# A kernel that multiplies each sample by its subject's matrix: how the eight matrices are loaded

## The chip, the cores and the metric

The kernel runs on one core of a Trainium2 chip. The metric is the device time of one execution in microseconds (us). The profile is of one execution, taken by the hardware profiler.

## The reference

There are 128 samples of 128 x 1024 floats, eight matrices of 128 x 128 floats, and for each sample the number of its subject. Each sample is multiplied by the matrix of its subject, and the sample itself is added:

```python
B, C, D, T, N_SUBJECTS = (128, 128, 128, 1024, 8)
w = weights[subjects]
out = jnp.einsum('bct,bcd->bdt', x, w)
x = x + out
```

All data are float32. The samples are 67 MB in and 67 MB out; the matrices are 0.5 MB, as much as one sample.

## The kernel before

Four samples (H x G, two halves of two) make a turn, and there are 32 turns. The memory on the chip holds 12 slots, `x_all`, of one turn each (2 MB); turn `i` uses slot `i % 12`. Every engine follows an order written out by hand, with semaphores between them.

**Loads.** ScalarE's queue issues all loads (L200 to L204), one DMA for each sample, through the helper `transfer` (L59). A load splits a sample's 512 KB into 32 runs of 16 KB: one run holds four rows of the sample (`ROWS`), and it goes to four partitions. From turn 12 on, ScalarE waits at L202 until the slot has been emptied, that is, until the store of the turn 12 before has landed. ScalarE computes nothing.

**The matrices.** SP's queue issues two DMAs at the start: the subjects' numbers (L180) and the matrices (L181). L181 reads `weights` as `s c d` and writes it as `c s d`: partition `c` gets row `c` of each of the eight matrices, so each run is one row, 512 B, and there are 1024 of them. VectorE waits for them at L222.

**Order of the compute.** VectorE prepares an index of the subjects (L193 to L199). For each half turn it copies the two matrices that are needed from `w_all` into `ws` (`place`, L153), and TensorE multiplies (`multiply`, L162) after a wait for the copies (L157) and one for the loads (L158). VectorE then adds the product to the sample in its slot (`add`, L174, after the wait at L173). TensorE and VectorE run their turns in loops (L226 and L231). GpSimd (L206 to L211) passes on to TensorE that a turn's loads have landed. At the start TensorE multiplies zeros (L186; six records in the profile).

**Stores.** SP waits at L213 until all loads of turn 7 (`AHEAD` is 8) have landed, and then stores turn after turn, each after a wait for its additions (L217). The last turn is stored in pieces, and the very last sample at L238.

Of the kernel before, what the change touches and what calls it, by code (L numbers as in the profile page):

```python
# [30 lines left out]
G = 2  # L31
H = 2
# [3 lines left out]
SLOTS = 12  # L36
# [5 lines left out]
DMA = 16  # L42

IDLE = 3

ROWS = 4

ALIGN = 4096
QUEUES = {mybir.EngineType.SP: "qSPDynamicHW", mybir.EngineType.Activation: "qActDynamicHW"}
# [2 lines left out]
def transfer(nc, engine, out, in_):  # L52

    later, nc._always_lower_symbolic_ap = nc._always_lower_symbolic_ap, False
    ins, outs = engine.lower_ap_dma(in_), engine.lower_ap_dma(out)
    nc._always_lower_symbolic_ap = later
    return engine.add_instruction(  # L59
        mybir.InstDMACopy(  # L60
            name=nc.get_next_instruction_name(),
            engine=engine.engine,
            ins=ins,
            outs=outs,
            mode="Copy",
            cce_op=ALU.bypass,
            queue=QUEUES[engine.engine],
        )
    )
# [3 lines left out]
def kernel(  # L73
# [7 lines left out]
    nc = tc.nc  # L81
    B, C, T = x.shape
    S, _, D = weights.shape
    NT = B // (G * H)

    def sbuf(name, *shape, dtype=F32):
        return ctx.enter_context(nc.sbuf_tensor(name, list(shape), dtype)).ap()
# [5 lines left out]
    x_all = sbuf("x_all", C, SLOTS * H * G * T)  # L93
# [1 line left out]
        x_all[:, i * H * G * T : (i + 1) * H * G * T].rearrange("c (q t) -> c q t", t=T)  # L95
        for i in range(SLOTS)
    ]
    w_all = sbuf("w_all", C, S, D)
    ws = [sbuf(f"w{i}", C, 1, D) for i in range(H * G)]
    zeros = sbuf("zeros", C, N)  # L100
    given, near, wrap = (sbuf(name, 1, B, dtype=I32) for name in ("given", "near", "wrap"))
# [3 lines left out]
    ]  # L105

    s_given = tc.alloc_semaphore("s_given")
    s_wall = tc.alloc_semaphore("s_wall")
    s_index = tc.alloc_semaphore("s_index")
    s_zeros = tc.alloc_semaphore("s_zeros")  # L110
# [9 lines left out]
    def emptied(i):  # L120
        turns = i // SLOTS
        return DMA * (H * G + 1) * turns - (DMA * G if i >= SLOTS and i % SLOTS == 0 else 0)

    def load(engine, i, q):
        transfer(
            nc,
            engine,
            xs[i % SLOTS][:, q, :],
            x[i * H * G + q].rearrange("(a r) t -> a (r t)", r=ROWS),
        ).then_inc(s_head if i * H * G + q < G else s_slot[i % SLOTS], DMA)  # L130

    def store(i, q0, q1):
        b = i * H * G
        transfer(
            nc,
            nc.sync,
            out[b + q0 : b + q1].rearrange("g d t -> d g t"),
            xs[i % SLOTS][:, q0:q1, :].rearrange("d (o g) t -> d o (g t)", g=min(G, q1 - q0)),
        ).then_inc(s_slot[i % SLOTS], DMA)

    def subjects_of(i):
        _, subject = nc.values_load_multi_w_load_instructions(
            index[0:1, i] if isinstance(i, slice) else index[0:1, bass.ds(i * (H * G), H * G)],
            engines=[mybir.EngineType.DVE],
            min_val=0,
            max_val=S - 1,
            skip_runtime_bounds_check_because="the index is clamped on the chip above",
        )
        return subject

    def place(h, subject):
        for q in range(h * G, (h + 1) * G):
            copy = nc.vector.tensor_copy(ws[q], w_all[:, bass.ds(subject[q], 1), :])  # L153
        copy.then_inc(s_go, 1)

    def multiply(slot, h):
        nc.tensor.wait_ge(s_go, 1).then_inc(s_go, -1)  # L157
        nc.tensor.wait_ge(s_ready, 1).then_inc(s_ready, -1)  # L158
        for q in range(h * G, (h + 1) * G):
            for t in range(0, T, N):  # L160
                at = slot * (H * G * T) + (q * T + t)
                mm = nc.tensor.matmul(  # L162
                    ps[h][:, q % G, t : t + N],
                    ws[q][:, 0, :],
                    x_all[:, bass.ds(at, N)],
                    start=True,
                    stop=True,
                )
        mm.then_inc(s_product, 1)

    def add(slot, h):
        mine = x_all[:, bass.ds(slot * (H * G * T) + h * G * T, G * T)]
        nc.vector.wait_ge(s_product, 1).then_inc(s_product, -1)  # L173
        nc.vector.tensor_tensor(  # L174
            mine, ps[h].rearrange("d g t -> d (g t)"), mine, ALU.add
        ).then_inc(s_added, 1)

    with tc.tile_critical():  # L178

        nc.sync.dma_start(given, subjects.rearrange("(o b) -> o b", o=1)).then_inc(s_given, DMA)  # L180
        nc.sync.dma_start(w_all, weights.rearrange("s c d -> c s d")).then_inc(s_wall, DMA)  # L181

        nc.vector.memset(zeros, 0.0).then_inc(s_zeros, 1)  # L183
        nc.tensor.wait_ge(s_zeros, 1)
        for _ in range(IDLE):
            nc.tensor.matmul(  # L186
                ps[P_SLOTS - 1][:, G - 1, :N], zeros[:, :D], zeros, start=True, stop=True
            )

        nc.vector.memset(index[:, B:], 0).then_inc(s_index, 1)  # L193
        nc.vector.wait_ge(s_given, DMA)
        nc.vector.tensor_scalar(near, given, -S, S - 1, ALU.max, ALU.min).then_inc(s_index, 1)  # L195
        nc.vector.wait_ge(s_index, 2)
        nc.vector.tensor_scalar(wrap, near, 0, S, ALU.is_lt, ALU.mult).then_inc(s_index, 1)  # L197
        nc.vector.wait_ge(s_index, 3)
        nc.vector.tensor_tensor(index[:, :B], near, wrap, ALU.add).then_inc(s_index, 1)  # L199
        for i in range(NT):  # L200
            if i >= SLOTS:
                nc.scalar.wait_ge(s_slot[i % SLOTS], emptied(i))  # L202
            for q in range(H * G):
                load(nc.scalar, i, q)  # L204

        for i in range(NT):  # L206
            if i == 0:
                nc.gpsimd.wait_ge(s_head, DMA * G).then_inc(s_ready, 1)
                nc.gpsimd.wait_ge(s_slot[0], DMA * G).then_inc(s_ready, 1)
            else:  # L210
                nc.gpsimd.wait_ge(s_slot[i % SLOTS], emptied(i) + DMA * H * G).then_inc(s_ready, H)  # L211

        nc.sync.wait_ge(s_slot[AHEAD - 1], DMA * H * G)  # L213
        for i in range(NT):
            for h in range(H):
                if i == NT - 1 or h == H - 1:
                    nc.sync.wait_ge(s_added, i * H + h + 1)  # L217
                    store(i, h * G if i == NT - 1 else 0, (h + 1) * G - (i * H + h == NT * H - 1))


        nc.vector.wait_ge(s_index, 4)
        nc.vector.wait_ge(s_wall, DMA)  # L222
        subject = subjects_of(slice(0, H * G))
        for h in range(H):
            place(h, subject)
        with nc.vector.Fori(0, NT) as turn:  # L226
            subject = subjects_of(turn + 1)
            for h in range(H):
                add(turn % SLOTS, h)
                place(h, subject)  # L230
        with nc.tensor.Fori(0, NT) as turn:  # L231
            for h in range(H):
                multiply(turn % SLOTS, h)
# [39 lines left out]
```

## Time and profile before

| | us |
|---|---|
| median of 3 runs | 323.39 |
| lowest and highest | 323.35, 323.67 |
| the profiled execution | 323.44 |
| its span, first to last instruction | 321.7 |
| TensorE's matmuls with samples (L162) | 239.6 busy |
| VectorE's additions (L174) | 146.7 busy, 2.29 each |
| VectorE's copies of matrices (L153) | 23.2 busy, 0.22 each |

The profile page has the span cut into 40 slices of 8 us, with each engine's busy share in tenths; the DMA rows have the mean busy share of the 16 DMA engines and what they moved. Windows give the same for any stretch of time. A line such as `ACTq L59 DMA_DIRECT2D ... x24` stands for 24 DMA issues by ScalarE's queue: its first number is when they began, the second how long they took together. q1 is SP's queue and q10 is ScalarE's. The trace also records every DMA packet, with its start, duration and size, and the times at which a transfer's semaphore increments landed; where the text speaks of packet records and landings, it means these.

### The profile page before, as it was taken

How to read it: one execution, taken by the hardware profiler on the slowest of the kernel's cores; microseconds unless marked ns; L12 is line 12 of the kernel's file. 1: busy time of each engine (PE TensorE's matmuls, PEld its weight loads, DVE VectorE, ACT ScalarE, POOL GpSimd, SP SyncE). 2: the span in 40 equal slices, each digit the busy share in tenths (PEclk: the TensorE clock that was granted, in tenths of full speed). 3: DMA queues.
4: the chain of work that ended last, by engine and by line, in shares of the span. 5: the costliest groups of instructions: out<-in, count | busy, mean ns of one | idle time of the engine just before them, and what ended most of it. 6: DMA issues, size and time to landing. Idle time of an engine off the chain costs nothing. (4 is left out here: it accounts for less than half of the span.)

```text
span 321.7 us, 2380 instructions
## 1 busy us (share of the span) xinstructions
PE 244.1 (76%) x518; PEld 101.0 (31%) x518; DVE 165.7 (52%) x202; POOL 0.2 (0%) x4
## 2 busy tenths in 40 slices
PE   5999999999999999959499684986959779300000
PEld 2434444443444444424143231432423234000000
DVE  2267776777677677736627465371754707500000
POOL 0000000000000000000000000000000000000000
PEclk9799999999999999979879999897998959755555
DMA  7999999999999999999999999999999999999997
GB/s 281 426 428 426 424 424 408 421 437 418 421 438 428 422 418 426 439 427 423 424 418 425 434 435 413 426 433 427 428 418 425 440 417 421 426 430 425 427 428 309
DMA packets 16051, 134.76 MB, mean 419 GB/s; under 512 B 2609, under 2 KB 3634, under 8 KB 3890
## 3 DMA queue, kind: packets, MB, share of 16 engines
q1 hardware_dynamic: 9906, 67.64, 50.1%
q10 hardware_dynamic: 6144, 67.12, 49.6%
q14 instruction: 1, 0.01, 0.0%
HBM read 67.63 MB, written 67.11 MB: 419 GB/s over the span
## 5 line engine op out<-in xcount | busy, mean ns | idle before, releaser
L162 PE MATMUL ps<-x_all,w 128*128 x512 | 239.6, 626 | 30.2 <-PEq L158 27.1
L174 DVE TENSOR_TENSOR x_all<-ps,x_all 128x2048 f32 x64 | 146.7, 2292 | 106.9 <-DVEq L173 106.9
L162 PEld LDWEIGHTS ps<-x_all,w 128*128 128x128 f32 x512 | 99.3, 199 | 170.5 <-issue 169.7
L153 DVE COPY w<-w_all 128x128 f32 x132 | 23.2, 219 | 4.3 <-DMA w_all<-in_L_cond_weights_dram 4.3
L186 PE MATMUL ps<-zeros 128*128 128x512 f32 x6 | 4.4, 897 | 1.7 <-DVE zeros L183 1.7
L186 PEld LDWEIGHTS ps<-zeros 128*128 128x128 f32 x6 | 1.7, 304 | 3.6 <-issue 1.9
L183 DVE MEMSET zeros<- 128x512 f32 x1 | 0.5, 485 | 1.0 <-SPq L178 1.0
L195 DVE TENSOR_SCALAR near<-given 1x128 int32<-1x128 int32 x1 | 0.2, 217 | 0.6 <-DMA given<-in_itok_B_dram 0.6
L199 DVE CUSTOM_DVE_ANT_0 index<-near,wrap 1x256 uint16<-1x256 uint16 x1 | 0.3, 280 | 0.0
L197 DVE TENSOR_SCALAR wrap<-near 1x128 int32<-1x128 int32 x1 | 0.2, 215 | 0.0
L260 POOL MEMSET const-bfloat16-1.0<- 128x1 bf16 x1 | 0.1, 101 | 0.0
L260 POOL MEMSET const-uint8-127<- 128x1 uint8 x1 | 0.1, 101 | 0.0
L260 POOL MEMSET const-float32-0.0<- 128x1 f32 x1 | 0.1, 98 | 0.2 <-issue 0.2
L260 POOL MEMSET const-float32-1.0<- 128x1 f32 x1 | 0.1, 98 | 0.0
L260 DVE BASE_LOAD x1 | 0.0, 21 | 0.1
L193 DVE MEMSET index<- 1x4 int32 x1 | 0.1, 62 | 0.0
## 6 DMA issues: line engine op xcount, KB each, us to landing
x_all<-in_x_dram ACTq DMA_DIRECT2D x128, 512.0 KB, 10.7
out_dram<-x_all SPq DMA_DIRECT2D x31, 2048.0 KB, 54.8
out_dram<-x_all SPq DMA_DIRECT2D x1, 1024.0 KB, 26.0
out_dram<-x_all SPq DMA_DIRECT2D x2, 512.0 KB, 21.0
w_all<-in_L_cond_weights_dram SPq DMA_DIRECT2D x1, 512.0 KB, 5.1
given<-in_itok_B_dram SPq DMA_DIRECT2D x1, 0.5 KB
```

The lines of the kernel that those rows point to most:

```text
L153: copy = nc.vector.tensor_copy(ws[q], w_all[:, bass.ds(subject[q], 1), :])
L162: mm = nc.tensor.matmul(ps[h][:, q % G, t : t + N], ws[q][:, 0, :], x_all[:, bass.ds(at, N)], start=True, stop=True,)
L174: nc.vector.tensor_tensor(mine, ps[h].rearrange("d g t -> d (g t)"), mine, ALU.add).then_inc(s_added, 1)
L183: nc.vector.memset(zeros, 0.0).then_inc(s_zeros, 1)
L186: nc.tensor.matmul(ps[P_SLOTS - 1][:, G - 1, :N], zeros[:, :D], zeros, start=True, stop=True)
L193: nc.vector.memset(index[:, B:], 0).then_inc(s_index, 1)
L195: nc.vector.tensor_scalar(near, given, -S, S - 1, ALU.max, ALU.min).then_inc(s_index, 1)
L197: nc.vector.tensor_scalar(wrap, near, 0, S, ALU.is_lt, ALU.mult).then_inc(s_index, 1)
L199: nc.vector.tensor_tensor(index[:, :B], near, wrap, ALU.add).then_inc(s_index, 1)
L260: nc = _bacc.Bacc("TRN2", target_bir_lowering=False, num_devices=1)
```

## The change

SP no longer loads the matrices. ScalarE's queue loads them with one more `transfer` right behind the four loads of turn 0, in the same form as a sample: all of `weights` as one flat row of floats, cut into 32 runs of 16 KB, each over four partitions. In this form, partition `p` of `w_runs` holds rows 8p to 8p + 7 of the 1024 rows, and not row `p` of each matrix.

Three steps sort them. VectorE transposes `w_runs` into `w_turned` in blocks of 32 x 32; ScalarE copies 16 blocks (of 32 partitions and 256 floats each) from `w_turned` to `w_moved`, from any group of 32 partitions to any other; VectorE transposes `w_moved` back into `w_runs`, of which `w_all` is now a view. `w_turned` and `w_moved` lie in the space of slot 11.

ScalarE does its copies ahead of the loads of turn 6 (`EARLY`), after a wait for the first transposition; ahead of the loads of turn 11 it waits for the second one. VectorE does both transpositions before its first `place`, and between them waits for all 16 copies.

```diff
+EARLY = 6
+
+BLOCK = 32
...
-    w_all = sbuf("w_all", C, S, D)
+
+    RUN = S
+    PER = BLOCK * RUN // C
+    BLOCKS = C // BLOCK
+    w_runs = sbuf("w_runs", C, S * D)
+    w_all = w_runs.rearrange("c (s d) -> c s d", s=S)
+
+    spare = x_all[:, (SLOTS - 1) * H * G * T :]
+    w_turned, w_moved = (spare[:, i * S * D : (i + 1) * S * D] for i in range(2))
...
+    s_moved = tc.alloc_semaphore("s_moved")
...
-        nc.sync.dma_start(w_all, weights.rearrange("s c d -> c s d")).then_inc(s_wall, DMA)
...
         for i in range(NT):
+            if i == EARLY:
+                nc.scalar.wait_ge(s_wall, DMA + 1)
+                for a in range(BLOCKS):
+                    for b in range(BLOCKS):
+                        nc.scalar.copy(
+                            w_moved[b * BLOCK : (b + 1) * BLOCK, :].rearrange(
+                                "l (a m h k j) -> l a h m k j", a=BLOCKS, m=PER, j=RUN, k=BLOCK // RUN
+                            )[:, a],
+                            w_turned[a * BLOCK : (a + 1) * BLOCK, :].rearrange(
+                                "l (j h m b k) -> l b h m k j", j=RUN, m=PER, b=BLOCKS, k=BLOCK // RUN
+                            )[:, b],
+                        ).then_inc(s_moved, 1)
+            if i == SLOTS - 1:
+                nc.scalar.wait_ge(s_wall, DMA + 2)
             if i >= SLOTS:
                 nc.scalar.wait_ge(s_slot[i % SLOTS], emptied(i))
             for q in range(H * G):
                 load(nc.scalar, i, q)
+            if i == 0:
+                transfer(
+                    nc,
+                    nc.scalar,
+                    w_runs,
+                    weights.rearrange("s c d -> (s c d)").rearrange("(a r) -> a r", r=ROWS * T),
+                ).then_inc(s_wall, DMA)
...
         nc.vector.wait_ge(s_index, 4)
         nc.vector.wait_ge(s_wall, DMA)
+        nc.vector.transpose(w_turned, w_runs).then_inc(s_wall, 1)
+        nc.vector.wait_ge(s_moved, BLOCKS**2)
+        nc.vector.transpose(w_runs, w_moved).then_inc(s_wall, 1)
+        nc.vector.wait_ge(s_wall, DMA + 2)
         subject = subjects_of(slice(0, H * G))
```

## The prediction

> **What bounds the kernel now.** I read the page's slices first.
>
> ```profile
> PE 244.1 (76%) x518; PEld 101.0 (31%) x518; DVE 165.7 (52%) x202; POOL 0.2 (0%) x4
> ...
> PE   5999999999999999959499684986959779300000
> ...
> DMA  7999999999999999999999999999999999999997
> GB/s 281 426 428 426 424 424 408 421 437 418 421 438 428 422 418 426 439 427 423 424 418 425 434 435 413 426 433 427 428 418 425 440 417 421 426 430 425 427 428 309
> ```
>
> The 16 DMA engines are full from the first slice to the last, at about 425 GB/s, while TensorE has gaps from slice 18 on and nothing to do in the last five. 134.76 MB have to move whatever the order, so the end moves only if (a) the transfers start earlier or later, (b) they occupy the engines for a different time, or (c) the engines run dry. The start is where the change sits, so next come the windows there.
>
> ```profile
> core 0: us, PE busy (x) PEld busy (x) DVE busy (x) POOL busy (x), PEclk, DMA share, GB/s
> 0.00:2.20 2.20, 0.54 (x1) 0.50 (x2) 0.51 (x3) 0.20 (x4) 1.00 0.00 0
> 2.20:4.00 1.80, 1.80 (x3) 0.67 (x2) 0.71 (x3) 0.00 (x0) 1.00 0.94 297
> 4.00:5.50 1.50, 1.50 (x4) 0.53 (x2) 0.00 (x0) 0.00 (x0) 1.00 1.22 383
> 5.50:6.50 1.00, 0.59 (x2) 0.00 (x0) 0.00 (x0) 0.00 (x0) 1.00 1.04 432
> 6.50:16.50 10.00, 8.20 (x15) 3.60 (x16) 3.14 (x7) 0.00 (x0) 0.83 1.01 429
> ```
>
> No packet moves before 2.2 us. From 4.0 to 5.5 us the matrices move: a share above 1 (packets overlap) at only 383 GB/s, where 16 KB packets later give 429. The queues in the first 10 us:
>
> ```profile
> q10 hardware_dynamic: 220, 2.56, 64.3%
> q1 hardware_dynamic: 1042, 0.52, 17.6%
> ```
>
> q1 is SP's queue, and 17.6% of 10 us is 1.76 us of all 16 engines for 0.52 MB. Then ScalarE's queue, which issues the loads and will carry the new work:
>
> ```profile
> 0.90 0.53 ACTq L59 DMA_DIRECT2D x_all<-in_x_dram  x1
> ...
> 15.79 1.63 ACTq L59 DMA_DIRECT2D x_all<-in_x_dram  x2
> 16.53 4.42 ACTq L59 DMA_DIRECT2D x_all<-in_x_dram  x3
> 19.90 26.13 ACTq L59 DMA_DIRECT2D x_all<-in_x_dram  x22
> ```
>
> The first 24 issues take 0.645 us each (15.6 us); near 17.4 us one takes 2.4 us, and the 22 after it 1.19 us each: the queue is full, with some 15 loads ahead of the engines. Last, what waits for the matrices and for compute:
>
> ```profile
> 7.31 0.63 DVE L153 COPY w<-w_all 128x128 f32 x4 [4.31 <-DMA w_all<-in_L_cond_weights_dram]
> 8.30 7.96 PE L162 MATMUL ps<-x_all,w 128*128 x14 [2.21 <-PEq L158]
> ...
> 44.80 33.34 SPq L59 DMA_DIRECT2D out_dram<-x_all  x7
> ```
>
> Real matmuls start at 8.30 us, and the first store leaves only at 44.80, held by the wait at L213.
>
> **The change part by part.** *The load of the matrices* (L181 out; behind slot 0's four loads on ScalarE's queue in). The packet records show load 0 leaving the engines at 4.02 us (mean of its last 16 packets), load 1 entering at 5.61 (mean of its first 16), and the matrices' 1024 packets of 512 B, 27 ns each, in between: 1.59 us occupied. Two successive loads stand 1.22 us apart (6.85, 8.07, 9.29, 10.51). Moved in 32 packets of 16 KB, the matrices take one such step: 1.59 - 1.22 = **0.37 us saved**, with 0.02 us that load 1 loses beside the last small packets 0.39. Bounds: by bytes, (429 - 383)/429 x 1.5 us = 0.16; by packet time, 1.75 - 1.22 = 0.53 (without overlap). I take 0.38, the starts of neighbouring loads, as they are what all later transfers follow.
>
> A rule speaks against this: the Trainium skill (DMA: Bandwidth & Descriptors, Specifications) puts line rate at 512 B and above, so 512 B runs would lose nothing and the sum would be 0. The 383 against 429 GB/s in this trace contradicts it.
>
> *Issue.* ScalarE issues one more DMA (0.645 us) and SP one fewer (0.42 us). Loads 1 to 3 and the matrices are issued at 1.46, 2.10, 2.74 and about 3.4 us; load 0 needed 1.32 us from issue to first packet (0.90 to 2.22), so they are ready at 2.8 to 4.7 and their turns come at 4.0 to 7.7. Nothing.
>
> *ScalarE's stop at slot 6.* 25 issues end at 0.90 + 25 x 0.645 = 17.0 us. The matrices land where the fourth load does now, 10.34 less 0.38 = about 10.0. No row has a transposition; over 1024 columns the nearest are COPY (219 ns for 128: 1.75 us) and the memset (485 ns for 512: 0.97); the addition (2292 ns for 2048) gives 1.15. I take 1.2; the first is over at 11.2, before ScalarE looks. No row has a ScalarE copy either. The line through COPY and memset gives 0.31 us for 256 columns; bounds 0.22 (COPY) and 2.29 (addition), so 3.5 to 37 us for 16. I take 0.4 to 0.5 with a set-up ahead of the first, 8 us in all: ScalarE is free at 25. Behind it wait the loads from slot 6 on. By 17.0 the engines have taken 1 + (17.0 - 4.02)/1.22 = 11.6 of the 25; the 13.4 left last 16.3 us, to 33.4. A new load must be issued 1.32 us ahead, by 32.0, so the stop may last 15 us. Cost 0; the cover is the queue's backlog, with 7 us left.
>
> *Later compute.* The second transposition ends at about 26.2; from the landing to the first placement (6.49 to 7.31) and on to the first matmul (8.29) took 1.8 us, so TensorE starts at about 28 rather than 8.3: 19.5 us later. Slots are added every 7.05 us (42.21 less 35.16), from 19.7 now, from 39.2 then. Store 0 is held until 44.8 anyway (5.6 us of cover). The engines turn to store 1 when store 0 has landed, at 62.0 (ScalarE's reload of that slot follows at once); slot 1 would be added at 46.3. Later stores land at 74, 86, 98, 108, about 10 to 12 us apart, more than 7.05, so the cover only grows. TensorE catches up with the loads: slot 24 is added at 211.0 now, at 39.2 + 24 x 7.05 = 208 then; the 27.1 us that it idles at L158 swallow the 19.5. Loads of turn 11, whose space is borrowed, are issued from 41.7 on, 15 us after the second transposition. Cost 0 throughout.
>
> **Sum:** the profiled execution took 323.44 us (span 321.7); 323.44 - 0.38 = 323.06. The median of the runs is 0.05 lower, so I predict **323.0**.
>
> **The rivals.** *The head of ScalarE's queue moves (slower).* The trace has no compute on ScalarE; its first copies may need an engine set-up, and if this stands ahead of the first load (0.90) rather than ahead of the copies, every transfer starts later by as much: there is no cover, since the engines move nothing before 2.2. Rows bound it by 0.02 us (BASE_LOAD) and 2.29 (the longest instruction); the middle, 1.15, gives 323.0 + 1.15 = 324.2. It decides from 0.38 us. For: L260 puts other set-up at the start. Against: nothing needs it before slot 6. The Trainium skill (ScalarE: Activation LUTs, What ACT_TABLE_LOAD costs) gives 1.283 us for a table load, by which the time would be 324.3, but places it right before the first ACTIVATE, where the backlog hides it; no run here shows either yet.
>
> *The queue runs dry (slower).* From 15 us of stop. At 1.2 us a copy, half of the upper bound, it lasts 19 us: 323.0 + 4.2 = 327. Strided reads of 32 partitions could do that; VectorE's rows give no sign of it.
>
> *The gap stays (slower).* If load 1's descriptors, not the small packets, were late at 5.61, the matrices come on top: 323.4 + 1.22 = 324.6. For: load 1 was issued at 1.46, over 4 us before. Against: load 0 needed 1.32, and the engines were full throughout.
>
> *More is won.* Load 0's packets took 0.83 us in the mean against 0.61 later, two deep: 0.43 us. If SP's descriptors for 1024 pieces cause it, the time is 323.0 - 0.43 = 322.6. Against: its slowest packets started at 2.2, before the first small one at 3.9.
>
> **How the numbers follow.** Forecast 0.73, set-up ahead 0.10, dry queue 0.05, gap stays 0.04, more won 0.08. About 0.2%, 0.65 us, is what a measurement of this kernel can tell from no change: the forecast's saving is 0.12% and lies within it. Faster: all but a little of the 0.08 reaches only -0.8, and the forecast's own upper bound adds about 0.12: 0.19 together. Slower: most of 0.10 + 0.05 + 0.04, 0.18. The rest, 0.63, within. The likeliest case's own range is 322.6 to 323.3 (0.8 to 0.1 saved); the whole range takes in the set-up's middle with 0.2 on top: 322.3 to 324.4, leaving out the dry queue, the staying gap and a long set-up, about 0.12.
>
> **What would show it.** Right: no 512 B packets but the few of the indices, 32 more of 16 KB; windows at 429 GB/s from 4.0 us; slot 1's first load entering at about 8.9 us instead of 9.3; ScalarE's copies between 17 and 25 us and the DMA row without a dent around 33; matmuls from about 28 us; stores from about 44.4; slots 24 on as before. Wrong: a first load issued later than 0.90; GB/s falling between 28 and 40 us; a hole between the first two loads; a dent after 45 us because stores wait for additions.

## The result, and the profile after

| | before | after |
|---|---|---|
| median of 9 runs, us | 323.61 | 324.61 |
| lowest and highest | 323.31, 323.88 | 324.09, 325.58 |
| ratio, with its 95% interval | | 1.0034 (1.0022 to 1.0045) |
| the profiled execution, us | 323.44 | 324.82 |
| its span | 321.7 | 323.0 |

The changed kernel is 1.0 us slower, where 0.38 us faster was forecast. The slices of its page:

```profile
PE   5001999999999999999999999996969779200000
...
ACT  0085000000000000000000000000000000000000
...
DMA  7999999999999999999999999999999999999996
GB/s 244 422 426 424 430 429 416 436 416 429 431 418 427 426 424 429 437 421 425 426 419 425 433 422 425 426 431 422 427 434 413 435 423 423 426 426 425 428 426 260
```

TensorE starts late (the second and third slices are empty), ScalarE has work, and the DMA row stays full throughout: neither ScalarE's stop nor the late compute left the engines dry. What changed stands in the first slice (244 GB/s, 281 before) and in the last (260, 309 before). First the head, in windows of the changed kernel:

```profile
core 0: us, PE busy (x) PEld busy (x) DVE busy (x) ACT busy (x) POOL busy (x), PEclk, DMA share, GB/s
4.00:5.50 1.50, 1.50 (x3) 0.53 (x2) 0.00 (x0) 0.00 (x0) 0.00 (x0) 1.00 1.42 371
5.50:7.50 2.00, 0.71 (x2) 0.00 (x0) 0.00 (x0) 0.00 (x0) 0.00 (x0) 1.00 0.75 287
7.50:10.00 2.50, 0.00 (x0) 0.00 (x0) 0.00 (x0) 0.00 (x0) 0.00 (x0) 0.71 0.95 393
```

and the same stretches before:

```profile
4.00:5.50 1.50, 1.50 (x4) 0.53 (x2) 0.00 (x0) 0.00 (x0) 1.00 1.22 383
5.50:7.50 2.00, 0.59 (x2) 0.00 (x0) 0.19 (x2) 0.00 (x0) 1.00 1.08 453
7.50:10.00 2.50, 1.70 (x2) 0.84 (x3) 0.44 (x4) 0.00 (x0) 0.66 1.00 426
```

After the change 287 GB/s were moved from 5.5 to 7.5 us, where it was 453. A window counts a packet, with all of its time, where it begins, so a share of 1.42 followed by 0.75 means that packets that began before 5.5 us took long. The packet records say which. For each transfer, in the order of the packets, this is the mean start of its first 16 packets in us, with the mean and longest duration of its 32 packets in ns:

```
          load 0           load 1           load 2           load 3           matrices        load 4
before    2.37 (827,1260)  5.61 (612,619)   6.85 (611,615)   8.07 (612,618)   (4.0 to 5.6)    9.29 (612,616)
after     2.35 (845,1280)  4.04 (697,1135)  5.44 (983,2080)  7.40 (674,1028)  8.74 (624,769)  9.99 (615,654)
```

Load 1 enters at 4.04 us, where the prediction put it, right behind load 0. But loads 1, 2 and 3 take 1.40, 1.96 and 1.34 us instead of 1.22 each. Eight of load 2's packets, which began between 5.18 and 5.35 us, took 1.8 to 2.1 us. The matrices themselves take 1.25 us, where 1.22 was forecast.

The last stretches, before and then after (the share is of all 16 engines):

```profile
319.00:319.50 0.50, 0.00 (x0) 0.00 (x0) 0.00 (x0) 0.00 (x0) 0.50 1.00 410
319.50:320.00 0.50, 0.00 (x0) 0.00 (x0) 0.00 (x0) 0.00 (x0) 0.50 0.21 82
320.00:320.50 0.50, 0.00 (x0) 0.00 (x0) 0.00 (x0) 0.00 (x0) 0.50 0.02 8
320.50:321.00 0.50, 0.00 (x0) 0.00 (x0) 0.00 (x0) 0.00 (x0) 0.50 0.00 0
```

```profile
319.00:319.50 0.50, 0.00 (x0) 0.00 (x0) 0.00 (x0) 0.00 (x0) 0.00 (x0) 0.50 1.00 410
319.50:320.00 0.50, 0.00 (x0) 0.00 (x0) 0.00 (x0) 0.00 (x0) 0.00 (x0) 0.50 0.61 246
320.00:320.50 0.50, 0.00 (x0) 0.00 (x0) 0.00 (x0) 0.00 (x0) 0.00 (x0) 0.50 0.25 98
320.50:321.00 0.50, 0.00 (x0) 0.00 (x0) 0.00 (x0) 0.00 (x0) 0.00 (x0) 0.50 0.10 41
321.00:321.70 0.70, 0.00 (x0) 0.00 (x0) 0.00 (x0) 0.00 (x0) 0.00 (x0) 0.50 0.06 23
```

The engines stop one after another, and the time ends with the last. Averaged over the 16, their work is over at 319.68 us before and at 320.10 after (319 us plus a sixteenth of the packet time that lies behind 319). The last packet ends at 320.28 and 321.64, so the last engine is 0.60 us behind the mean before and 1.54 after. The difference of 1.36 us between the two executions is thus 0.42 in the mean and 0.94 in the step between the engines. The mean is made up so: the matrices save 0.34 (1.25 us instead of 1.59), loads 1 to 3 lose 1.02 (4.70 us instead of 3.68), and 16 KB packets' time above 612 ns each ("excess" below, per engine) between 40 and 60 us, when the stores start, costs 0.15 instead of 0.46: -0.34 + 1.02 - 0.31 = 0.37 of the 0.42.

### The profile page after: what moved, and what is told of

Read it like the earlier page. It is cut to its first block, busy times and chain, and to the rows that moved or that the text cites. A ratio compares the mean times of both kernels' runs of the same rounds, so it can differ in the third digit from the quotient of the medians.

```text
span 323.0 us, 2399 instructions
## 1 busy us (share of the span) xinstructions
PE 239.1 (74%) x518; PEld 99.3 (31%) x518; DVE 168.2 (52%) x204; ACT 11.1 (3%) x17; POOL 0.2 (0%) x4
## 5 line engine op out<-in xcount | busy, mean ns | idle before, releaser
L175 PE MATMUL ps<-x_all,w 128*128 x512 | 234.6, 616 | 35.8 <-DVE w L166 25.3
L175 PEld LDWEIGHTS ps<-x_all,w 128*128 128x128 f32 x512 | 97.6, 196 | 172.8 <-issue 171.8
L166 DVE COPY w<-w_runs 128x128 f32 x132 | 23.2, 219 | 0.8 <-DVE w_runs L262 0.8
L217 ACT COPY x_all<-x_all 32x256 f32<-32x256 f32 x16 | 9.8, 614 | 0.4
L262 DVE STREAM_TRANSPOSE w_runs<-x_all 128x1024 f32<-128x1024 f32 x1 | 1.2, 1247 | 16.4 <-ACT x_all L217 16.4
L260 DVE STREAM_TRANSPOSE x_all<-w_runs 128x1024 f32<-128x1024 f32 x1 | 1.2, 1245 | 8.0 <-DMA w_runs<-in_L_cond_weights_dram 8.0
L217 ACT ACT_TABLE_LOAD x1 | 1.3, 1283 | 17.1 <-issue 17.1
## 6 DMA issues: line engine op xcount, KB each, us to landing
x_all<-in_x_dram ACTq DMA_DIRECT2D x128, 512.0 KB, 10.8
```

The costliest lines, as they stand in the source:

```text
L175: mm = nc.tensor.matmul(ps[h][:, q % G, t : t + N], ws[q][:, 0, :], x_all[:, bass.ds(at, N)], start=True, stop=True,)
L217: nc.scalar.copy(w_moved[b * BLOCK : (b + 1) * BLOCK, :].rearrange("l (a m h k j) -> l a h m k j", a=BLOCKS, m=PER, j=RUN, k=BLOCK // RUN) ...
L260: nc.vector.transpose(w_turned, w_runs).then_inc(s_wall, 1)
L262: nc.vector.transpose(w_runs, w_moved).then_inc(s_wall, 1)
```

## The experiments

In this order: which part of the change costs, what the matrices' transfer did for the loads behind it, and whether the second queue or the small packets did it. All are compared with runs of the kernel before on the same chip. For each there are, from its trace, the time by which ten transfers of 512 KB had been moved (matrices included; the mean end of the last 16 packets of the tenth), and how far the last engine was behind the mean at the end.

| kernel | ten moved, us | last behind mean, us | median, us | ratio (95%) |
|---|---|---|---|---|
| before | 15.41 | 0.60 | 323.61 | |
| after | 16.11 | 1.54 | 324.61 | 1.0034 (1.0022 to 1.0045) |
| e1_again: after | 15.97 | 0.87 | 324.36 | 1.0024 (1.0014 to 1.0034) |
| e2_no_sort: no sorting | 16.12 | 1.20 | 324.35 | 1.0022 (1.0012 to 1.0032) |
| e3_late: before, compute late | 15.37 | 1.07 | 323.59 | 1.0001 (0.9991 to 1.0011) |
| e4_small_fifth: 512 B, fifth | 16.47 | 1.49 | 324.69 | 1.0027 (1.0018 to 1.0037) |
| e5_ninth: matrices ninth | 16.21 | 1.31 | 324.65 | 1.0028 (1.0017 to 1.0038) |
| e6_small_second: 512 B, second | 15.83 | 0.87 | 324.22 | 1.0025 (1.0014 to 1.0035) |
| e7_flat_sp: 16 KB on SP | 15.22 | 0.88 | 323.89 | 1.0013 (1.0004 to 1.0022) |
| e8_rows4k: samples 1, 2 in 4 KB | 16.27 | 1.53 | 324.75 | 1.0035 (1.0023 to 1.0048) |
| e9_two_queues: sample 1 on SP | 15.33 | 0.87 | 323.84 | 1.0010 (1.0001 to 1.0019) |
| e10_pause: issue pauses | 16.46 | 1.38 | 324.86 | 1.0036 (1.0022 to 1.0049) |
| e11_sp_no_sort: 16 KB on SP, no sorting | 15.29 | 0.67 | 323.62 | 1.0008 (0.9996 to 1.0019) |
| e12_before: before | 15.43 | 0.76 | 323.52 | 1.0000 (0.9991 to 1.0009) |

### Once more, and each part alone

e1_again is the changed kernel itself.

> The changed kernel once more. In the first trace the bulk of the transfers ran as before; what differed was the head (packets of the first loads slower: 1.51 us per engine above their usual duration in the first 20 us, against 0.42 before), the start of the stores (0.09 against 0.41 us between 40 and 60 us) and the step between the engines at the end (the last store's 16 landings 2.06 us apart, against 0.87). HEAD (16 KB packets right behind load 0 are slow, small ones cover it) and STEP (late compute lets the engines fall out of step): all three come again, time 324.6. CHANCE: slow packets or the spread differ by more than 0.5 us from the first trace, and the time with them.

The slow head came again (excess in the first 20 us 1.10, beside 1.55 in the first trace and 0.47 before; the expectations count it from 616 ns; ten transfers moved at 15.97): six of load 2's packets, begun at 5.14 to 5.23 us, took 1.4 to 1.7 us. The step at the end was smaller, 0.87, and so was this execution's time, 323.99. The slow head came in both traces, so it belongs to the kernel; how far the last engine falls behind varies from one execution to the next.

e2_no_sort takes the sorting out and leaves the transfer:

```diff
-            if i == EARLY:
-                nc.scalar.wait_ge(s_wall, DMA + 1)
...
-            if i == SLOTS - 1:
-                nc.scalar.wait_ge(s_wall, DMA + 2)
...
-        nc.vector.transpose(w_turned, w_runs).then_inc(s_wall, 1)
-        nc.vector.wait_ge(s_moved, BLOCKS**2)
-        nc.vector.transpose(w_runs, w_moved).then_inc(s_wall, 1)
-        nc.vector.wait_ge(s_wall, DMA + 2)
```

> The matrices in 32 runs of 16 KB as the fifth sample, without the two transpositions, the 16 copies and their waits, so the samples are multiplied by unsorted rows; compute starts at about 11 us instead of 31. HEAD: the slow first packets stay (1.5 us of excess), the loss at the start of the stores comes back (0.4): 323.6 - 0.37 + 1.07 = 324.3. STEP: the spread falls to 0.9 us. If late compute alone is what costs: 323.2, as forecast for the load by itself.

324.35, the same as with the sort (324.36 in e1_again), and the same head. The transpositions, the copies, ScalarE's stop and the late compute cost nothing that shows here. The loss at the start of the stores did not come back (0.14 us), so late compute is not what spared it.

e3_late is the other half, late compute in the kernel before (its matmuls with samples start at 31.57 us, beside 31.49 in the changed kernel):

```diff
         nc.vector.wait_ge(s_wall, DMA)
+        nc.vector.wait_ge(s_slot[4], DMA * H * G)
```

> The kernel before, with VectorE's first copies of matrices held back until turn 4 has landed (about 30 us), so that compute is as late as in the changed kernel and nothing else moves. STEP: the stores' landings fall 2 us apart, time 323.6 - 0.3 (start of the stores) + 0.9 = 324.2. HEAD alone: spread 0.9, head as before, 323.3.

323.59 beside 323.49: late compute costs nothing that shows, as forecast. Its trace had the last engine 1.07 us behind, more than the 0.60 and 0.76 of the kernel before; the ratio's interval leaves no room for more than 0.4 us of it.

e4_small_fifth leaves the form of the matrices as it was and moves only their place:

```diff
-        nc.sync.dma_start(w_all, weights.rearrange("s c d -> c s d")).then_inc(s_wall, DMA)
...
                 load(nc.scalar, i, q)
+            if i == 0:
+                nc.scalar.dma_start(w_all, weights.rearrange("s c d -> c s d")).then_inc(s_wall, DMA)
```

> The kernel before, with the matrices still in 1024 runs of 512 B, but on ScalarE's queue behind the four loads of turn 0; no sorting. If full loads right behind load 0 are slow (HEAD), loads 1 to 3 now are and the small packets cover nothing: excess 1.5 us, 324.7. If the slow head belongs to the 16 KB form of the matrices: excess 0.4, 323.6.

324.69: the whole loss, without a single 16 KB run of the matrices. Its windows show the same hole and then, from 7.5 us, the small packets:

```profile
4.00:5.50 1.50, 1.50 (x4) 0.44 (x2) 0.00 (x0) 0.00 (x0) 1.00 1.34 339
5.50:7.50 2.00, 0.39 (x1) 0.00 (x0) 0.00 (x0) 0.00 (x0) 1.00 0.68 270
7.50:10.00 2.50, 0.00 (x0) 0.00 (x0) 0.00 (x0) 0.00 (x0) 0.58 0.93 324
```

So what costs is that the matrices no longer come between load 0 and load 1. That left two readings: small packets pass through this stretch unharmed, or a transfer of the second queue does.

### Small packets or a second queue

e5_ninth moves the matrices of the changed kernel behind turn 1 (`if i == 1:` instead of `if i == 0:`).

> The changed kernel with the matrices behind turn 1's loads, as the ninth transfer. WINDOW (whatever full loads enter from some 4 to 5.5 us on, behind load 0, are slow, until about 7.5 us): the same slow packets in loads 1 and 2, excess 1.0 to 1.5 us, 324.4. If the matrices' place as the fifth has a part in it (its descriptors are made while load 2 runs): excess 0.4, 323.2.

324.65, with an excess of 0.91 us, just under the 1.0 to 1.5 expected: their place as the fifth doesn't make the slow head. With eight loads of samples ahead of them, 287 GB/s were moved from 5.5 to 7.5 us, as in the changed kernel.

e6_small_second puts the small runs between loads 0 and 1, but on ScalarE's queue:

```diff
                 load(nc.scalar, i, q)
+                if i == 0 and q == 0:
+                    nc.scalar.dma_start(w_all, weights.rearrange("s c d -> c s d")).then_inc(s_wall, DMA)
```

> The kernel before, with the matrices in 1024 runs of 512 B on ScalarE's queue, right behind load 0. COVER (small packets behind load 0 are not slowed and the full loads come after the window): excess 0.4, load 1 enters at 5.4 us or later, 323.5. If it was the second queue, SP's, that kept the packets fast: excess 1.0 to 1.5, 324.5.

324.22, with an excess of 0.87 us. The time can't be told from e4_small_fifth's (ratio 1.0025 beside 1.0027); the head lies between the two kernels that move the matrices in the same form, with ten transfers at 15.83 beside 15.41 before and 16.47 in e4_small_fifth. The 512 B packets kept to 27 ns in the mean, but loads 1 and 2 behind them still had packets of up to 1.53 and 1.08 us. Small packets in that place spare some of the head, but not all of it.

e7_flat_sp issues the 16 KB runs where the kernel before issued the matrices, on SP's queue:

```diff
         nc.sync.dma_start(given, subjects.rearrange("(o b) -> o b", o=1)).then_inc(s_given, DMA)
+        transfer(
+            nc,
+            nc.sync,
+            w_runs,
+            weights.rearrange("s c d -> (s c d)").rearrange("(a r) -> a r", r=ROWS * T),
+        ).then_inc(s_wall, DMA)
...
-            if i == 0:
-                transfer(
...
```

> The changed kernel, with the matrices' 32 runs of 16 KB on SP's queue where the kernel before issues them. COVER: full packets run behind load 0, so they are slow as in the changed kernel, excess 1.0 to 1.5, 324.4. SECOND QUEUE: excess 0.4, 323.2.

The hole is gone, with full packets behind load 0:

```profile
4.00:5.50 1.50, 1.50 (x3) 0.60 (x2) 0.00 (x0) 0.00 (x0) 0.00 (x0) 1.00 1.09 437
5.50:7.50 2.00, 1.64 (x2) 0.07 (x1) 1.25 (x1) 0.00 (x0) 0.00 (x0) 1.00 0.95 401
7.50:10.00 2.50, 0.00 (x0) 0.00 (x0) 0.00 (x0) 0.00 (x0) 0.00 (x0) 1.00 0.98 413
```

The excess is 0.44 us, and ten transfers were moved at 15.22 us, the earliest of all and 0.19 us earlier than in the kernel before. The time, 323.89, is not the 323.2 expected: it is 0.4 us above the kernel before, with the last engine 0.88 us behind the mean.

e8_rows4k has samples 1 and 2 in runs of 4 KB, on ScalarE's queue (`r=1 if i == 0 and q in (1, 2) else ROWS` in `load`).

> The changed kernel, with samples 1 and 2 in 128 runs of 4 KB (a row each) instead of 32 of 16 KB. COVER: packets of 4 KB pass through the window at their usual 0.16 us each, excess 0.4, the forecast saving appears: 323.1, below the kernel before. If any load behind load 0 is slow, or only packets as small as 512 B are spared: 324.4.

324.75. The packets of 4 KB were slowed like the large ones (those begun from 5.0 to 5.25 us took 0.73 us in the mean instead of 0.16).

e9_two_queues moves one sample of the changed kernel to SP's queue; the matrices stay the fifth on ScalarE's:

```diff
         nc.sync.dma_start(given, subjects.rearrange("(o b) -> o b", o=1)).then_inc(s_given, DMA)
+        load(nc.sync, 0, 1)
...
             for q in range(H * G):
-                load(nc.scalar, i, q)
+                if (i, q) != (0, 1):
+                    load(nc.scalar, i, q)
```

> The changed kernel, with sample 1 loaded by SP's queue at the start instead of ScalarE's; the matrices stay the fifth on ScalarE's. TWO QUEUES (the first loads of one queue alone run into slow packets between 5 and 7.5 us; a transfer of the other queue in between spares them): excess 0.4 us, work of the engines over at about 319.4, time 323.3 to 323.8. If only the matrices' transfer on SP spares them: excess 1.0 to 1.5, 324.4.

```profile
4.00:5.50 1.50, 1.50 (x3) 0.60 (x2) 0.00 (x0) 0.00 (x0) 0.00 (x0) 1.00 1.02 393
5.50:7.50 2.00, 1.65 (x2) 0.07 (x1) 0.00 (x0) 0.00 (x0) 0.00 (x0) 1.00 0.97 410
7.50:10.00 2.50, 0.00 (x0) 0.00 (x0) 0.00 (x0) 0.00 (x0) 0.00 (x0) 1.00 1.01 419
```

410 GB/s instead of 287 from 5.5 to 7.5 us, no packet over 0.94 us behind load 0, ten transfers at 15.33, and 323.84. The excess in the first 20 us is 0.71, where 0.4 was expected, and the engines' work is over at 319.74 in the mean (319.4 expected). One sample issued by the other queue takes away the slow spell and 0.5 to 0.8 us of the loss (ratio 1.0010 beside 1.0024 and 1.0034). With e7_flat_sp this decides for the second queue and against the size of the packets.

One reading isn't separated from it. In both kernels SP's transfer also makes ScalarE's next load begin later: at 5.3 us, 3.9 us after its issue, instead of 4.0, 2.6 us after it. If the time since the start were what counts, load 1 of e6_small_second, begun at 5.65, should be fast, and it had packets of 1.53 us. If the time since the issue were (3.6 us there), SP's own 16 KB packets, begun from 2.4 us after their issue on, should be slow, and they took 0.67 and 0.68 us in the mean. So the delay explains it only if SP's queue differs from ScalarE's; no run has all the first loads on SP's queue.

e10_pause asks whether ScalarE's issues, made while loads 1 and 2 run, slow them (`nc.scalar.wait_ge(s_head, DMA * G)` ahead of turn 1's loads).

> The changed kernel, with ScalarE waiting, before it issues turn 1's loads (the sixth transfer and on), until the first two loads have landed, at about 6 us. ISSUE (the issues made between 3.4 and 6 us slow the packets that run then): excess 0.4, 323.5. If the slow packets belong to a time after the start or to loads 1 and 2 themselves: excess 1.0 to 1.5, 324.4. If the pause lets the queue run dry (three transfers, 3.7 us, lie ahead at 6 us): a gap near 8 us.

No: nothing was issued from 4.0 to 7.2 us, and packets begun from 4.2 to 5.6 us still took up to 2.02 us. No gap followed (426 GB/s from 7.5 to 10 us), and the time was 324.86. The first load issued after the pause, at 7.16 us, had four slow packets of its own (begun at 10.8 us, 1.33 to 1.63 us each), so slow packets are not tied to the first 8 us of the execution.

### What is left

e11_sp_no_sort is e7_flat_sp less the sorting.

> The matrices in 32 runs of 16 KB on SP's queue at the start, without transpositions, copies and their waits, so the samples are multiplied by unsorted rows. With the sort this took 323.89. If ScalarE's stop or the late compute widens the step between the engines: 323.3, below the kernel before by the 0.15 to 0.3 us that the shorter load is worth. If neither does: 323.9 again.

323.62, within its interval the same as before, with the last engine 0.67 us behind. With the sorting it was 323.89, but the two intervals overlap, so that the sort costs something here isn't settled.

e12_before is the kernel before once more, unchanged.

> The kernel before, unchanged, for a second trace: head excess 0.3 to 0.5 us, excess between 40 and 60 us 0.4 to 0.5, the last engine 0.6 us behind the mean at the end. If the last number alone differs by 0.3 us or more, the step between the engines is a matter of each execution and not of the kernel.

It agrees with the first trace: head excess 0.38 (0.47), ten transfers at 15.43 (15.41), 0.76 us behind (0.60).

What a transfer on SP gains at the head is partly lost later. The excess between 40 and 60 us, when the stores start, is 0.45 to 0.67 us in the six traces with a transfer on SP (and 0.50 in e6_small_second), and 0.10 to 0.15 in the other seven. What sets it is not shown.

None of the twelve is faster than the kernel before, and no experiment points to a version that would be. The 0.3 to 0.4 us that e7_flat_sp and e9_two_queues stay above it are not explained.

## Why the prediction was wrong

**The load of the matrices.** This is the step that failed: "Moved in 32 packets of 16 KB, the matrices take one such step: 1.59 - 1.22 = **0.37 us saved**". The matrices do take 1.25 us. What was wrong is the sum around it: it put loads 1 to 3 behind load 0 at 1.22 us each, a step read from loads that in the kernel before only start at 5.6 us, with SP's transfer between. With all of it on ScalarE's queue they take 4.70 us instead of 3.68, and slot 1's first load (load 4 above) enters at 9.99 us, where 8.9 was named as the sign of being right. The step treated the transfer on SP as a cost only, and it was also what kept the loads around it fast (ratios in the table; e4_small_fifth without it: 324.69; e7_flat_sp and e9_two_queues with a transfer on SP: 323.89 and 323.84).

**The rule on 512 B.** The rule of the Trainium skill weighed there (512 B and above at line rate) is contradicted again by e4_small_fifth, where the small runs took about 1.6 us for 512 KB (load 3 enters at 7.52, load 4 at 10.34, less 1.22 for load 3), though they are not what decided.

**Issue.** "Nothing" held for the time at which the transfers were ready: load 1 entered at 4.04 as load 0 left. That a load which is ready in time may still run slowly was not considered.

**ScalarE's stop.** Right in its cost, wrong in its sizes.

```profile
L217 ACT COPY x_all<-x_all 32x256 f32<-32x256 f32 x16 | 9.8, 614 | 0.4
...
L217 ACT ACT_TABLE_LOAD x1 | 1.3, 1283 | 17.1 <-issue 17.1
```

```profile
17.06 1.28 ACT L217 ACT_TABLE_LOAD   x1 [17.06 <-issue]
18.35 7.64 ACT L217 COPY x_all<-x_all 32x256 f32<-32x256 f32 x12
25.39 1.12 ACTq L63 DMA_DIRECT2D x_all<-in_x_dram  x2
...
27.93 0.61 ACT L217 COPY x_all<-x_all 32x256 f32<-32x256 f32 x1
```

These are groups and the order of time on ScalarE. A copy took 614 ns where 400 to 500 was taken. The set-up stands right ahead of the first copy, at 17.06, so the rival that put it ahead of the first load is out. The Trainium skill (ScalarE: Activation LUTs, What ACT_TABLE_LOAD costs) gives about 1283 ns for such a load, and the trace has 1283. The queue issues again at 25.4 us, near the 25 forecast, but only since it runs ahead of the last copies, which end at 28.5: the agreement is luck. The queue did not run dry: 433 GB/s from 25 to 35 us.

**Later compute.** Matmuls start at 31.5 us instead of the 28 forecast, because the copies end 3.5 us later than taken, and this costs nothing that shows (e3_late and e2_no_sort). Slot 24 is added at 212.7 us, beside 211.0 before.

```profile
30.58 0.63 DVE L166 COPY w<-w_runs 128x128 f32 x4 [0.76 <-DVE w_runs L262]
31.49 2.07 PE L175 MATMUL ps<-x_all,w 128*128 x2 [25.29 <-DVE w L166]
```

**The other rivals.** The gap did not stay: load 1 entered at 4.04. That this rival gave 324.6, the time that was measured, is luck. Load 0 was not faster (845 ns a packet, 827 before). A slow spell of the loads themselves was not among the rivals at all.

**The step between the engines.** The sum went by the mean of the engines, but the time ends with the last one. Where ScalarE's queue had the head alone, it was 0.87 to 1.54 us behind the mean (eight traces); with a transfer on SP, 0.60 to 1.07 (six). In the first trace this is the larger part, 0.94 of 1.36 us. It does not come straight from the head. By the 16 landings of each transfer, the last engine is 0.56 us behind the mean for loads from 25 to 35 us in the changed kernel and 0.69 in the one before. The difference arises once loads and stores mix: in the same order it is 1.5 and 1.1 us for most loads from 53 to 100 us, 3.2 to 3.6 and 1.0 to 1.5 us for the last stores beside loads (234 to 268 us), and 1.6 and 0.6 for the stores alone after that. What makes it is open, and so is why packets begun near 5 us are slow when one queue has the head alone; later, the same queue alone runs at about 1.22 us a load, but for the second spell in e10_pause.

## What to carry to other kernels

A transfer that looks like mere cost at the start may stand in a place that matters: before it is moved, ask what runs in its place, and do not take the pace of later transfers for that of the first few. Two queues on the same engines were worth 0.6 to 0.9 us in the first ten transfers here (15.22 and 15.33 beside 15.97 and 16.11). In this kernel, whose DMA engines are full throughout, compute that started 23 us later cost nothing that could be measured, and the end was set by the last of the 16 engines, not by their mean.

## What the runs showed of the hardware that was not expected

- With one queue alone, 16 KB packets begun about 4 to 5.7 us after the start took up to 2.2 us instead of 0.61; with a transfer from the other queue right behind the first load, none after that load took more than 1.02 us (six traces). The Trainium skill (DMA: Bandwidth & Descriptors, Issuing engines are not separate DMA queues) says that issuing on several engines saves only the time of issue; in the first 16 us of this kernel it saved 0.6 to 0.8 us of transfer (e9_two_queues, 15.33, beside 15.97 and 16.11).
- A transposition of 128 x 1024 floats in 32 x 32 blocks took 1.25 us on VectorE.
- ScalarE's queue issued DMAs while copies ahead of them in its order were still to run: the first at 25.39 us, the last copy ended at 28.54.
